# Perceiver layer on one core: half of the causal masks by ScalarE and GpSimd, one division for two quads, weights in halves, projections in four column groups

## The chip, the core and the metric

The kernel runs on one core of a Trainium2 chip. A core has five engines with a queue each: PE (TensorE, matmuls, and PEld for its weight loads), DVE (VectorE), ACT (ScalarE), POOL (GpSimd) and SP (SyncE, which issues most DMAs here). Each works through its own queue in order and waits on semaphores for the others. Matmul results land in PSUM[...]; what GpSimd works on here lies in SBUF. The metric is the device time of one execution in microseconds, as the median of several runs.

## The reference

x is 4 batches of 256 tokens with 256 features; the context is 4 x 4096 x 256. Everything is fp32. Three residual blocks follow each other:

```python
x = x + xattn(layernorm(x), ctx, ctx, ...)          # 16 heads of 16, 4096 keys, softmax
x = x + attn(layernorm(x), ...)                     # causal linear attention
x = x + ffn(layernorm(x), w_gate, w_up, w_down)     # silu(gate) * up, int32 weights / 127
```

The second block maps normalised queries and keys through 64 exponential features per head, and sums causally:

```python
kv_cur = jnp.cumsum(kv_prod, axis=2) + kv_state[:, :, None]
k_cur = jnp.cumsum(k_ch, axis=2) + k_state[:, :, None]
ctx = jnp.einsum('bhtf,bhtfd->bhtd', q_ch, kv_cur)
den = jnp.maximum(jnp.einsum('bhtf,bhtf->bht', q_ch, k_cur), 1e-06)
out_ch = ctx / den[..., None]
```

The kernel computes it as masked attention: for each head the scores of features against features, keys down and queries across, are set to zero where the key comes later, and then multiplied with the values and a column of ones, which gives the denominator.

## The kernel before, in words

**Cross-attention** (`cross_attention`, from L569) takes most of the time. Work is cut into units of one batch and one *quad* (four heads), 16 units of 16 steps each. A step works on 256 keys: matmuls for the maxima of a later unit (pm, L708, reduced by DVE at L715), the shifted scores (pt, L745), the exponentials on ACT (L750), and the product with the values (pav, L765), which DVE adds up at L775. In between, half of a key or value item is projected from the context (pk L642, pv L672). Each of these halves is written as matmuls of 32 output columns, four side by side: `pk[32 * j : 32 * j + 32, :]`. The trace shows such a matmul as two records of form 128*32, a full one as two of form 128*128, and one with 32 contraction rows as 32*128.

At the end of a unit, `finish` divides by the sums (`normalise`, L785), sends the rows through eight small DMAs on SP into another layout (xo<-on, L806), turns them (`turn`, px L815) and, for every second unit, projects them (`project`, py L823) and adds to the residual xr (L826).

**The causal part's beginning** is laid into the last steps of that loop (`start_causal`, L285): for batches 0 to 2, layernorm, transposition (tr L202), queries and keys (pqk L211, with the squares sq on GpSimd, L217), values (pv L229), normalisation of queries and keys (`qk_normed` L253, with `inverse_root`, L120, a chain of small DVE instructions), and the first features. Each of these calls uses two or four full 128-column matmuls.

**The causal part** (from L513) is an order written out by hand. It has 16 quads (`attend(n)`, n = 4 * batch + quad). Step n of the last loop queues, on all engines: `values` of quad n-1 (po L430, copied to avT by ACT, L435), `scores` of quad n (four heads, two at a time, pa L411 and L416, each masked by DVE: at = pa * mask, L421), `divide` of quad n-1 (two transpositions of avT into pt_o, L442, then den, reciprocal and product on DVE, L444 to L446), in steps 0, 2, 4, 8 and 10 `features` of two later quads (pf L275, clipped by DVE at L281, exponential by ACT at L282, a factor by GpSimd at L283), and then the step's entries in `fills`. These hold the conversion of the three int32 weights on ACT (`weight`, L394: steps 1, 2 and 3; each starts the load of the next on SP), the last unit's `turn15` and `project15` (steps 2 and 3), layernorm, queries, keys and values of batch 3 (norm3 in step 3, qk3 in 4 and 5, v3 in 5), and the output projection and feed-forward of each batch (tr_o L460, py L466, tr_z L483, pg and pu L492, pd L504) from step 4 on.

All PSUM tiles come from one pool of eight banks in turn (`bank`, L179), so a tile waits until the tile eight places earlier has been read.

```python
normalise()
weight_load(0)
fills[1] += [lambda: weight(0)]
fills[2] += [turn15, lambda: weight(1)]
fills[3] += [project15, norm3, lambda: weight(2)]
early = {0: 6, 2: 8, 4: 10, 8: 12, 10: 14}
```

## Time and profile before

| | |
|---|---|
| median of 3 runs | 1228.5 us (1228.21 to 1228.61) |
| profiled execution | 1229.02 us, its span 1227.3 us |
| PE / PEld busy | 1193.0 us (97%) / 807.0 us (66%) |
| DVE / ACT / POOL busy | 927.9 us (76%) / 673.0 us (55%) / 60.2 us (5%) |
| at<-pa,mask on DVE (L421) | 64 times, 550 ns each |
| at the end of the loop: last pav | 1065.9 to 1069.2 us |
| last instruction on DVE (o<-pd,xr) | 1224.1 us |

The span runs from the first to the last instruction of the profiled execution; the time of an execution includes what lies around it. An engine's busy time says nothing by itself of what a change is worth: the *chain* follows the work that ended last back to what released it, and shows which engine's time was the program's time at each place. Rows by stretch ("from:to length, PE busy (x instructions) ... PEclk, DMA share, GB/s") show where PE, which bounds the whole, has gaps. In a row of the timeline, the first number is the start, the second the duration, "x4" the number of instructions merged, and brackets hold the idle time before and what ended it.

### The profile page before, as it was taken

How to read it: one execution, taken by the hardware profiler on the slowest of the kernel's cores; microseconds unless marked ns; L12 is line 12 of the kernel's file. 1: busy time of each engine (PE TensorE's matmuls, PEld its weight loads, DVE VectorE, ACT ScalarE, POOL GpSimd, SP SyncE). 2: the span in 40 equal slices, each digit the busy share in tenths (PEclk: the TensorE clock that was granted, in tenths of full speed). 3: DMA queues.
4: the chain of work that ended last, by engine and by line, in shares of the span. 5: the costliest groups of instructions: out<-in, count | busy, mean ns of one | idle time of the engine just before them, and what ended most of it. 6: DMA issues, size and time to landing. Idle time of an engine off the chain costs nothing.

```text
span 1227.3 us, 42096 instructions
## 1 busy us (share of the span) xinstructions
PE 1193.0 (97%) x17712; PEld 807.0 (66%) x17712; DVE 927.9 (76%) x1823; ACT 673.0 (55%) x1394; POOL 60.2 (5%) x115
## 2 busy tenths in 40 slices
PE   7999999999999999999999999999999999959998
PEld 3566667666766676667666776677667755536777
DVE  6887777777777777777777777777788877577763
ACT  3456665566666655666656556655566546641311
POOL 4010000000000000000000000000001012120100
PEclk9999999999999999999999999999999999999999
DMA  6452331233123322332233213322232000020000
GB/s 208 135 192 67 101 114 56 80 105 106 64 79 89 116 71 63 103 119 72 60 102 106 86 58 91 103 90 73 86 105 91 5 1 4 2 80 1 10 9 18
DMA packets 57756, 95.78 MB, mean 78 GB/s; under 512 B 29024, under 2 KB 31712, under 8 KB 57568
## 3 DMA queue, kind: packets, MB, share of 16 engines
q1 hardware_dynamic: 56640, 92.44, 24.3%
q8 instruction: 140, 2.29, 0.8%
q10 hardware_dynamic: 416, 0.66, 0.2%
q14 instruction: 48, 0.39, 0.1%
q0 software_dynamic: 512, 0.00, 0.0%
HBM read 74.17 MB, written 1.05 MB: 61 GB/s over the span
## 4 chain that ended last, share of the span: by engine, by line
PE 92%; DVE 4%; ACT 1%; DMA 1%; issue 1%; SPq 0%; POOL 0%; DVEq 0%; ACTq 0%
PE pt L745 22%; PE pm L708 18%; PE pav L765 18%; PE pk L642 11%; PE pv L672 10%; PE pd L504 2%; PE pg L492 1%; PE pu L492 1%; PE pq L848 1%; PE pqk L211 1%; PE po L430 1%; PE pa L411 1%; PE py L823 1%; PE py L466 1%; DVE mx L715 1%; PE pf L275 1%
## 5 line engine op out<-in xcount | busy, mean ns | idle before, releaser
L715 DVE TENSOR_REDUCE mx<-pm 128x1 f32<-128x512 f32 x1024 | 635.6, 684 | 145.4 <-PE pm L708 145.3
L750 ACT ACTIVATE e<-pt 128x512 f32<-128x512 f32 x1024 | 529.2, 602 | 384.2 <-PE pm L708 359.6
L745 PE MATMUL pt<-qa,kt 32*128 32x256 f32 x4096 | 500.2, 388 | 1.3 <-DVE av L775 0.7
L708 PE MATMUL pm<-kt,qT 32*128 32x512 f32 x2048 | 494.6, 616 | 0.0
L745 PEld LDWEIGHTS pt<-qa,kt 32*128 32x128 f32 x4096 | 317.0, 184 | 117.2 <-ACT v L679 43.2
L765 PE MATMUL pav<-e,v 128*32 128x256 f32 x4096 | 269.8, 380 | 0.0
L708 PEld LDWEIGHTS pm<-kt,qT 32*128 32x128 f32 x2048 | 172.2, 184 | 15.5 <-issue 3.7
L765 PEld LDWEIGHTS pav<-e,v 128*32 128x32 f32 x4096 | 128.7, 110 | 73.9 <-ACT e L750 4.7
L775 DVE TENSOR_TENSOR av<-pav,av 128x256 f32<-128x256 f32 x240 | 101.7, 424 | 65.7 <-PE pav L765 65.4
L672 PE MATMUL pv<-wv_sb,ctx 128*32 128x128 f32 x4096 | 137.5, 276 | 0.0
L642 PE MATMUL pk<-ctx,wk_sb 128*32 128x256 f32 x2048 | 136.7, 388 | 0.0
L672 PEld LDWEIGHTS pv<-wv_sb,ctx 128*32 128x32 f32 x4096 | 104.2, 109 | 43.5 <-DVE mx L715 42.7
L642 PEld LDWEIGHTS pk<-ctx,wk_sb 128*32 128x32 f32 x2048 | 54.8, 110 | 67.1 <-DVE mx L715 39.0
L650 ACT ACTIVATE ku<-pk,bk_sb 128x256 f32<-128x256 f32 x128 | 63.2, 495 | 11.2 <-PE pk L642 9.9
L679 ACT COPY v<-pv 128x256 f32<-128x256 f32 x128 | 51.4, 402 | 9.9 <-PE pv L672 9.9
L802 POOL TENSOR_TENSOR on<-on,bv_sb 128x64 f32<-128x64 f32 x32 | 9.2, 308 | 820.5 <-DVE on L797 820.5
L421 DVE TENSOR_TENSOR at<-pa,mask 128x384 f32<-128x384 f32 x64 | 31.2, 550 | 7.0 <-PE pa L416 7.0
L282 ACT ACTIVATE kt<-kt,shift 128x512 f32<-128x512 f32 x32 | 22.4, 725 | 22.0 <-DVE kt L281 22.0
L281 DVE TENSOR_SCALAR kt<-pf,low,top 128x512 f32<-128x512 f32 x32 | 23.7, 803 | 3.9 <-PE pf L275 3.9
L492 PE MATMUL pg<-zT,wg 128*128 128x256 f32 x96 | 23.0, 382 | 0.7 <-ACT zT L484 0.7
L496 ACT ACTIVATE th<-pg 128x512 f32<-128x512 f32 x12 | 7.1, 594 | 29.8 <-PE pg L492 29.8
L492 PE MATMUL pu<-zT,wu 128*128 128x256 f32 x96 | 22.7, 379 | 0.0
(126 smaller groups left out, 565.6 us busy)
## 6 DMA issues: line engine op xcount, KB each, us to landing
ctx<-in_ctxT_dram SPq DMA_DIRECT2D x128, 512.0 KB
kt<-ku SPq DMA_DIRECT2D x508, 32.0 KB
xo<-on SPq DMA_DIRECT2D x128, 8.0 KB
xr<-in_x_dram SPq DMA_DIRECT2D x4, 256.0 KB
out_dram<-o SPq DMA_DIRECT2D x8, 128.0 KB
wqkv_sb<-in_wqkv_dram SPq DMA_DIRECT2D x1, 768.0 KB
w_i<-in_w_gate_dram SPq DMA_DIRECT2D x1, 768.0 KB
w_i<-in_w_up_dram SPq DMA_DIRECT2D x1, 768.0 KB
```

Source lines behind the costliest of these rows:

```text
L421: nc.vector.tensor_tensor(at, pa, mask, ALU.mult)
L492: nc.tensor.matmul(ps[:, i, :], lhsT=w[:, k, ns], rhs=zT[:, k, :], start=k == 0, stop=k == KC - 1)
L642: nc.tensor.matmul(pk[32 * j : 32 * j + 32, :], lhsT=wk_sb[:, k, m * P + 32 * j : m * P + 32 * j + 32], rhs=x[:, k, cs], start=k == 0, sto ...
L650: nc.scalar.activation(ku[:, cs], made.pop(), AF.Identity, bias=bk_sb[:, m : m + 1])
L672: nc.tensor.matmul(pv[32 * j : 32 * j + 32, i, :], lhsT=x[:, k, t0 + 32 * j : t0 + 32 * j + 32], rhs=wv_sb[:, k, m * P : (m + 1) * P], sta ...
L679: nc.scalar.copy(to.rearrange("p t (h d) -> p t h d", d=HD + 1)[:, :, :, :HD], made.pop().rearrange("p t (h d) -> p t h d", d=HD),)
L708: nc.tensor.matmul(pm, lhsT=qT[rows, q, t0 : t0 + P], rhs=kt[rows, c * CH : (c + 1) * CH], start=True, stop=True,)
L715: nc.vector.tensor_reduce(mx[:, i, j, c : c + 1], pm, AX.X, ALU.max)
L745: nc.tensor.matmul(pt[:, i, :], lhsT=kt[rows, ks], rhs=qa[rows, :], start=True, stop=True)
L750: nc.scalar.activation(e, pt, AF.Exp, scale=0.25)
L765: nc.tensor.matmul(pav[32 * h : 32 * h + 32, :], lhsT=v[:, t % KT, c0 : c0 + 32], rhs=es[n, h][:, i, :], start=i == 0, stop=i == 1,)
L775: nc.vector.tensor_tensor(avs[u], pav, avs[u], ALU.add)
```

## The change

Four things are changed.

1. A helper `product4` issues one product as four matmuls of 32 output columns each. pk and pv of the loop, which already did this, call it; new is that pqk (L211), pv of the causal part (L229) and py of the cross-attention (L823) do too.
2. Each int32 weight is loaded and converted in two halves, through a tile with two buffers. Two loads are queued after `normalise()`; the six conversions stand in steps 1 to 6, and each queues the load two places further on.
3. `divide` runs in every second step, for two quads: four transpositions into one bank, one den, reciprocal and product with twice the elements. avT gets three buffers.
4. Of the four scores of a quad, the first two are copied from PSUM by ACT, and GpSimd sets the two triangles of the copy to zero (`affine_select` over the blocks 0 and 2); the other two are multiplied by the mask on DVE as before.

The instructions of the other parts, and their order, stay as they are.

```diff
+    def product4(out, lhsT, rhs, **flags):
+
+        for j in range(4):
+            js = slice(32 * j, 32 * j + 32)
+            nc.tensor.matmul(out[js], lhsT=lhsT[:, js], rhs=rhs, **flags)
...
-                nc.tensor.matmul(
-                    ps, lhsT=zT[:, k, i * P : (i + 1) * P], rhs=rest[3][:, k, : 2 * D],
+                product4(
+                    ps, zT[:, k, i * P : (i + 1) * P], rest[3][:, k, : 2 * D],
                     start=k == 0, stop=k == KC - 1,
                 )
...
-                    nc.tensor.matmul(
-                        ps[:, i, :], lhsT=zT[:, k, i * P : (i + 1) * P], rhs=rest[3][:, k, 2 * D :],
+                    product4(
+                        ps[:, i, :], zT[:, k, i * P : (i + 1) * P], rest[3][:, k, 2 * D :],
                         start=k == 0, stop=k == KC - 1,
                     )
...
+    def weight_load(n):
+        i, half = divmod(n, 2)
+        w = ws[i].shape[1] // 2
+        src = (w_gate, w_up, w_down)[i][:, half * w : half * w + w, :]
+        coming[n] = work.tile([P, w, ws[i].shape[2]], I32, tag="w_i", name="w_i")
+        nc.sync.dma_start(out=coming[n], in_=src)
+
+    def weight(n):
...
+        nc.scalar.activation(
+            ws[i][:, half * w : half * w + w, :], coming.pop(n), AF.Copy, scale=(1.0, 0.5, 1.0)[i] / 127.0
+        )
+        if n + 2 < 6:
+            weight_load(n + 2)
...
                 for pa in pas:
                     at = work.tile([P, 3, P], F32, tag="at", name="at", bufs=8)
-                    nc.vector.tensor_tensor(at, pa, mask, ALU.mult)
+                    if part == 0:
+                        nc.scalar.copy(at, pa)
+                        nc.gpsimd.affine_select(
+                            out=at[:, 0:3:2, :], in_=at[:, 0:3:2, :], compare_op=ALU.is_ge, fill=0.0, base=0,
+                            pattern=[[0, 2], [1, P]], channel_multiplier=-1,
+                        )
+                    else:
+                        nc.vector.tensor_tensor(at, pa, mask, ALU.mult)
                     ats.append(at)
...
         def divide():
...
+            pt = bank([P, 2, 8, 32], "pt_o")
+            for m, oT in enumerate(got):
+                for i in range(2):
+                    nc.tensor.transpose(
+                        pt[:, i, 4 * m : 4 * m + 4].rearrange("p j r -> p (j r)"), oT[:, i * P : (i + 1) * P], ident
+                    )
+            got.clear()
+            den = work.tile([P, 2, 8], F32, tag="den", name="den")
             nc.vector.tensor_scalar(den, pt[:, :, :, HD], 1e-6, None, ALU.max)
             nc.vector.reciprocal(den, den)
...
-        weight_load(0)
+        for n in range(2):
+            weight_load(n)
...
+        for n in range(6):
+            fills[n + 1] += [lambda n=n: weight(n)]
+        fills[2] += [turn15]
+        fills[3] += [project15, norm3]
...
-            if n > 0:
+            if n > 0 and n % 2 == 0:
                 steps[n - 1][2]()
...
-                    nc.tensor.matmul(
-                        py, lhsT=oT[:, k, :], rhs=rest[1][:, k, :], start=k == 0, stop=k == KC - 1
-                    )
+                    product4(py, oT[:, k, :], rest[1][:, k, :], start=k == 0, stop=k == KC - 1)
```

More of the change, by code (lines that the diff above doesn't have):

```diff
@@ L363, in perceiver_layer @@
     finish = cross_attention(
-        tc, xr, load_x, load_rest, ctxT, wq_sb, bq_sb, wkP, bk_sb, wvP, eps, ident, layernorm, transposed,
+        tc, xr, load_x, load_rest, ctxT, wq_sb, bq_sb, wkP, bk_sb, wvP, eps, ident, layernorm, transposed, product4,
         qT, kts, lnp, bank, rest, start_causal)
@@ L386, in perceiver_layer @@
     ]
-    coming = []
-    def weight_load(i):
-        src = (w_gate, w_up, w_down)[i]
-        coming.append(load(src, list(ws[i].shape), "w_i", mybir.dt.int32, nc.sync, late))
-    def weight(i):
-        nc.scalar.activation(ws[i], coming[i], AF.Copy, scale=(1.0, 0.5, 1.0)[i] / 127.0)
-        if i + 1 < len(ws):
-            weight_load(i + 1)
+    coming = {}
+    def weight_load(n):
[5 more added lines that the diff above has]
+    def weight(n):
+        i, half = divmod(n, 2)
+        w = ws[i].shape[1] // 2
+        nc.scalar.activation(
[3 more added lines that the diff above has]
+            weight_load(n + 2)
+    got = []
     def attend(n):
         b, q = divmod(n, NQ)
-        ats, got = [], []
+        ats = []
         def scores():
@@ L433, in values @@
                     )
-            oT = work.tile([P, T], F32, tag="avT", name="avT")
+            oT = work.tile([P, T], F32, tag="avT", name="avT", bufs=3)
             nc.scalar.copy(oT, po)
@@ L438, in divide @@
         def divide():
-            oT = got.pop()
-            pt = bank([P, 2, 4, 32], "pt_o")
-            for i in range(2):
-                nc.tensor.transpose(pt[:, i].rearrange("p j r -> p (j r)"), oT[:, i * P : (i + 1) * P], ident)
-            den = work.tile([P, 2, 4], F32, tag="den", name="den")
+            pt = bank([P, 2, 8, 32], "pt_o")
[6 more added lines that the diff above has]
+            den = work.tile([P, 2, 8], F32, tag="den", name="den")
             nc.vector.tensor_scalar(den, pt[:, :, :, HD], 1e-6, None, ALU.max)
@@ L446, in divide @@
             nc.vector.tensor_tensor(
-                att[:, 2 * b : 2 * b + 2, 64 * q : 64 * q + 64].rearrange("p t (j d) -> p t j d", d=HD),
-                pt[:, :, :, :HD], den.unsqueeze(3).to_broadcast([P, 2, 4, HD]), ALU.mult,
+                att[:, 2 * b : 2 * b + 2, 64 * q - 64 : 64 * q + 64].rearrange("p t (j d) -> p t j d", d=HD),
+                pt[:, :, :, :HD], den.unsqueeze(3).to_broadcast([P, 2, 8, HD]), ALU.mult,
             )
@@ L519, in perceiver_layer @@
         norm3, turn3, qk3, sq3, v3, _ = causal_in(3)
-        fills[1] += [lambda: weight(0)]
-        fills[2] += [turn15, lambda: weight(1)]
-        fills[3] += [project15, norm3, lambda: weight(2)]
+        for n in range(6):
+            fills[n + 1] += [lambda n=n: weight(n)]
+        fills[2] += [turn15]
+        fills[3] += [project15, norm3]
         fills[4] += [turn3, lambda: qk3(0)]
@@ L569, in cross_attention @@
 def cross_attention(tc, xr, load_x, load_rest, ctxT, wq_sb, bq_sb, wkP, bk_sb, wvP, eps,
-                    ident, layernorm, transposed, qT, kts, lnp, bank, rest, start_causal):
+                    ident, layernorm, transposed, product4, qT, kts, lnp, bank, rest, start_causal):
     nc = tc.nc
@@ L640, in half @@
                 for k in range(KC):
-                    for j in range(4):
-                        nc.tensor.matmul(
-                            pk[32 * j : 32 * j + 32, :],
-                            lhsT=wk_sb[:, k, m * P + 32 * j : m * P + 32 * j + 32], rhs=x[:, k, cs],
-                            start=k == 0, stop=k == KC - 1,
-                        )
+                    product4(
+                        pk, wk_sb[:, k, m * P : (m + 1) * P], x[:, k, cs], start=k == 0, stop=k == KC - 1
+                    )
             def out(part):
@@ L670, in half @@
                     for k in range(KC):
-                        for j in range(4):
-                            nc.tensor.matmul(
-                                pv[32 * j : 32 * j + 32, i, :], lhsT=x[:, k, t0 + 32 * j : t0 + 32 * j + 32],
-                                rhs=wv_sb[:, k, m * P : (m + 1) * P], start=k == 0, stop=k == KC - 1,
-                            )
+                        product4(
+                            pv[:, i, :], x[:, k, t0 : t0 + P], wv_sb[:, k, m * P : (m + 1) * P],
+                            start=k == 0, stop=k == KC - 1,
+                        )
             def out(part):
@@ L822, in project @@
                 for k in range(KC):
-                    nc.tensor.matmul(
-                        py, lhsT=oT[:, k, :], rhs=rest[1][:, k, :], start=k == 0, stop=k == KC - 1
-                    )
+                    product4(py, oT[:, k, :], rest[1][:, k, :], start=k == 0, stop=k == KC - 1)
                 nc.vector.tensor_tensor(xr[:, t, :], py, xr[:, t, :], ALU.add)
```

## The prediction

> **What bounds the kernel now.** I read the page first (its slices, its chain), then busy time by stretches, then the chain and the engines' own timelines between 960 and 1228 us. The page's chain is 92% PE, and up to slice 35 PE is busy nine tenths or more: in the cross-attention loop, time is PE time, and only PE work taken out there counts. The end is different:

> ```profile
> core 0: us, PE busy (x) PEld busy (x) DVE busy (x) ACT busy (x) POOL busy (x), PEclk, DMA share, GB/s
> 130.00:900.00 770.00, 769.26 (x12659) 520.94 (x12652) 591.14 (x1054) 469.09 (x986) 7.45 (x26) 1.00 0.29 88
> ...
> 1080.00:1100.00 20.00, 11.78 (x118) 7.73 (x114) 14.13 (x44) 8.00 (x10) 3.42 (x6) 0.91 0.29 100
> 1100.00:1120.00 20.00, 15.96 (x106) 10.42 (x104) 14.04 (x40) 4.86 (x9) 3.99 (x6) 0.91 0.00 1
> 1120.00:1140.00 20.00, 19.37 (x143) 14.63 (x141) 18.04 (x47) 4.65 (x8) 1.41 (x3) 1.00 0.00 1
> ```

> From 1080 to 1120 PE idles 12.3 of 40 us and its clock is 0.91. Steps 0 to 7 of the causal part lie in 1070 to 1132; after that PE is full again (19.1 to 19.8 of 20 until 1200). The chain there, in order of time, says who holds PE up:

> ```profile
> 1077.67 4.33 DMA w_i<-in_w_gate_dram
> 1082.03 1.48 ACT wg L394
> 1083.51 0.27 ACT avT L435
> 1083.82 0.69 PE pt_o L442 x2
> 1084.51 2.06 PE pf L275 x16
> ...
> 1090.24 1.47 ACT wu L394
> 1091.70 0.27 ACT avT L435
> 1092.02 0.44 PE pt_o L442 x2
> 1092.45 0.88 PE py L823 x4
> ...
> 1098.01 1.86 DVE at L421 x4
> ...
> 1100.50 2.88 DVE kt L281 x4
> 1103.38 0.61 DVE zT L203
> 1104.03 3.68 PE pqk L211 x4
> ```

> A weight conversion on ScalarE waits for its DMA, the small copy avT waits behind it, the transposition pt_o waits for avT, and everything behind pt_o on PE waits too. Then VectorE is the chain, up to pqk, and again up to 1123.8, where values (po) takes 2.23 us instead of 0.86 because the masks come late. Two operations are also slow by themselves: pf 2.06 (1.07 at 1134.82) and pqk 3.68 (1.91 to 1.98 for the same two matmuls earlier). By stretches the granted clock is 0.50 from 1084 to 1086 and 0.53 from 1104 to 1106: 2.8 us lost, after PE pauses of 3.59 and 3.79 us.

> **Part 1, projections in column groups.** The same shape stands in the trace as pk and pav:

> ```profile
> 237.13 1.00 PE pk L642 x16
> 238.13 0.86 PE pav L765 x16
> 239.00 1.06 PE py L823 x4
> ```

> pk and pav are 8 calls of 32 columns each (two records a call), py two calls of 128; all stream the same number of columns. pav directly after pk costs 0.86; after a 32-row operation or a full 128-column one (at 985.82, 990.66, 996.59) it costs 1.00. The switch of form costs, not the number of calls. So py goes from 1.06 to 0.86 behind pav: 7 times 0.20 in the loop. pqk (1.91 to 1.98) plus pav (1.00) becomes 1.00 + 0.86 + 0.86 = 2.72: 6 times 0.23. L229's pv (1.92) plus pav becomes the same 2.72: 3 times 0.20. Sum 3.4; one pqk (1018) lies where VectorE is the chain (1016 to 1028), so I take **3.0**. [...] The row decides: 8 calls take 1.00, two take 1.06. Ends: 0 and 3.4.

> **Part 2, weights in halves.** SP still issues eight xo transfers first (until 1077.67), so the load starts no earlier. The whole load is seen after 4.36 us. By stretches of one us it moved at 276 and 406 GB/s from 1078.7 to 1080.7, so 393 KB are in at about 1080.0, and with the tail of 0.45 between the last bytes and ScalarE's start, the half is there at about 1080.5; the conversion halves to 0.74. avT of quad 1 then ends 1.5 + 0.7 = 2.2 us earlier. Ends: 0.7 (only the conversion) and 2.9. The other five halves have a whole step each for landing; the two buffers make SP wait, with nothing but later halves queued behind it until the first output.

> **Part 3, division for two quads.** Step 3 has no transposition any more. That was the wait of 2.57 us at 1092.02, for avT behind four exponentials and a whole conversion; py now waits only for the oT copy, behind VectorE's clips. The copy avT of quad 2 is needed a step later. Gain about 2.4 up to py. Transpositions stay 32 in number, 0.27 to 0.37 a pair; the form switch that is saved in even quads is paid by the next pg instead: nothing. VectorE saves 8 times den and reciprocal (0.16 + 0.20), off the chain except in steps 3 to 7.

> **Part 4, half of the masks.** VectorE loses 2 of 4 masks in each quad (pitch 0.465). ScalarE gains two copies 128x384 from PSUM: avT (128x256) takes 0.37, zT (128x512) 0.59, so 0.48 each. GpSimd gains two selects of 2x128. The nearest row is the mask's own making:

> ```profile
> 1069.77 0.54 POOL L375 TENSOR_SCALAR_AFFINE_SELECT mask<-mask 128x128 f32<-128x128 f32 x2
> ```

> 0.27 for 128 elements; for 256, between 0.4 (a fixed part as in L283, 0.48 for 256) and 0.54; I take 0.45. So these masks come about 0.9 us after the scores instead of 0.47, but a step is 6 us long, and values reads them a step later. What is queued behind the copies on ScalarE are avT, exponentials, conversions: 0.84 a step on an engine that is a quarter busy from 1100 on. In steps 1 and 3 the copies stand behind four exponentials (ended 1076.7 and 1090.3): po then waits about 3.1 and 2.0 us where it waited less, but that time was lost at pt_o in any case.
> Walking the engines' orders with these durations, VectorE's chain in step 4 is shorter by two masks less a longer division (0.7), form switches in step 5 give 0.2, and step 7's late masks vanish (0.63 wait + 1.4 stretch, 2.2 with their switch).

> **A price.** [...]

> ```profile
> 1020.92 2.13 DVE L253 TENSOR_TENSOR kt<-kt,nrm 128x512 f32<-128x512 f32 x2
> ...
> 1021.14 1.35 POOL L217 TENSOR_TENSOR sq<-kt 128x512 f32<-128x512 f32 x1 [10.05 <-DVE kt L215]
> ```

> against 1.28 and 1.04 apart. The selects of quad 3 fall into the root's small steps of norm3 (L131 to L133, two inputs), which are the chain: by the row 0.85[...]; I take **0.9** off. Ends 0 and 2. [...] The feed-forward's roots have some 3 us before their z is turned (tr_z stands behind 5.2 us of pd); the root of normed in step 5 has less, which is in the upper end.

> **Sum.** Up to py 2.2 + 2.4, less 0.1 for a changed wait: 4.5. Step 4: 0.7. Step 5: 0.2. Step 7: 2.2. That is 7.6. Less 0.9. Loop 3.0. The half clock cost 2.8; the pause before pqk stays about 3.7 us by the same walk, the first falls into pieces of 3.1 and 0.8; I count one short relapse of 1.0, so 1.8 won. Total 7.6 - 0.9 + 3.0 + 1.8 = **11.5 us**. The profiled execution took 1229.0 (span 1227.3), so 1217.5; the median of the runs is 0.5 lower: **1217.0**.

> **Rivals.**
> *The clock and the handover eat the middle.* Both pauses still bring the half clock (-1.8)[...]: 8.6 won, 1219.9. For it: the pause before pqk hardly shrinks. Against: shorter stalls of 2.57 and 2.06 left the clock at 1.00.
> *Column groups give nothing*[...], or the loop hides them: 8.5 won, 1220.0. For it: the loop's VectorE is busy three quarters. Against: the 0.14 between the two costs of pav.
> *GpSimd decides; slower.* All 32 masks pass it, in one strict order with 20 multiplications by fac, each 0.48, that the scores need. If a select of this two-block pattern costs 2 us instead of 0.45, two selects and the features fill the 6 us step and everything from step 2 on follows GpSimd: the walk's 7.6 is gone at 2.0 us, and with the loop's 3.0 the tie with before lies at 2.2; at 2.5 the end comes 8 us later than now in the causal part, 1228.5 + 8 - 3 = 1233.5. For it: spans on POOL are rough, and no row has this shape. Against: five times the nearest row.
> *The change doesn't do what it says*: the masks are needed so late that only PE counts, and weights land as late as before: about 1225.

> **Chances.** Forecast 0.64, clock and handover 0.13, no column gain 0.11, little of it 0.05, GpSimd 0.05, no change 0.02. Everything won (3.4 + 7.7 + 2.8) gives 1214.6; loop 1.0, middle 5.6, no clock gives 1222. Range 1214 to 1222. A difference under 0.2% (2.5 us) can't be told from none; faster 0.92, same 0.03, slower 0.05.

> **What will show it.** pav after pqk at 0.86 and py at 0.86; ScalarE's first conversion starting near 1080.5 less the loop's gain; no pt_o in odd steps and py about 5 us nearer to the loop's end; po of step 7 without a stretch; selects of about 0.45; clock 1.00 in the middle. Wrong would be: selects over 1 us, po waiting for GpSimd after step 8, or a loop that ends no earlier.

## The result, and the profile after

The changed kernel takes **1217.6 us** (median of 4 runs, 1216.87 to 1217.84) against 1228.55 for the kernel before on the same chip (4 runs, 1228.21 to 1228.62). The ratio is 0.991 with a 95% interval of 0.9893 to 0.9927: 11.0 us less, where 11.5 were forecast. The profiled execution took 1217.58 us with a span of 1215.9, 11.4 shorter than the span before.

The stretches of the causal part, in the same columns as before:

```profile
1080.00:1100.00 20.00, 13.87 (x132) 7.78 (x131) 14.33 (x38) 10.87 (x19) 7.87 (x15) 0.91 0.23 68
1100.00:1120.00 20.00, 19.95 (x194) 14.39 (x193) 17.84 (x54) 6.97 (x14) 3.39 (x7) 1.00 0.01 2
1120.00:1140.00 20.00, 19.44 (x160) 15.13 (x158) 13.60 (x37) 6.92 (x14) 3.48 (x8) 1.00 0.02 7
```

PE idles 6.2 us between 1080 and 1120, half of the 12.3 before (6.5, if the stretches are laid 2.8 us earlier, as the loop now ends), and of the two stretches with a clock of 0.91 one is left. GpSimd's busy time (the fifth pair) has more than doubled in the first row, from 3.42 to 7.87, without becoming full. The chain of waits over the same steps, shortened to the lines that answer to those of before:

```profile
1073.93 3.15 DMA w_i<-in_w_gate_dram
...
1077.85 0.36 ACT avT L458
...
1078.26 0.44 PE pt_o L465 x2
1078.69 1.11 PE pf L281 x16
...
1083.14 1.11 PE py L159 x16
...
1090.85 2.88 DVE kt L287 x4
1093.72 0.61 DVE zT L209
...
1094.38 3.46 PE pqk L159 x16
```

pt_o of quad 1 starts at 1078.26 instead of 1083.82, pf is back from 2.06 to 1.11, and py starts at 1083.14 instead of 1092.45 with no transposition just ahead of it. But pqk, two stages later, still takes 3.46, and VectorE is still the chain ahead of it. The timeline gives the same place from the side of the waits and of the new operations. First two rows of the kernel before, then the changed one:

```profile
1104.03 3.68 PE L211 MATMUL pqk<-wqkv_sb,zT 128*128 128x512 f32 x4 [3.79 <-DVE zT L203]
...
1123.78 2.23 PE L430 MATMUL po<-at,va 128*32 128x256 f32 x16 [0.63 <-DVE at L421]
```

```profile
1068.87 0.78 POOL L439 TENSOR_SCALAR_AFFINE_SELECT at<-at 128x256 f32<-128x256 f32 x2
...
1074.88 1.23 PE L453 MATMUL po<-at,va 128*32 128x256 f32 x16 [2.44 <-POOL at L439]
...
1077.10 0.84 ACT L405 ACTIVATE wg<-w_i 128x768 f32<-128x768 int32 x1 [2.36 <-DMA w_i<-in_w_gate_dram]
...
1085.42 1.23 PE L453 MATMUL po<-at,va 128*32 128x256 f32 x16 [1.21 <-POOL at L439]
...
1094.38 3.46 PE L159 MATMUL pqk<-wqkv_sb,zT 128*32 128x512 f32 x16 [3.97 <-DVE zT L209]
...
1113.40 1.00 PE L453 MATMUL po<-at,va 128*32 128x256 f32 x16
```

A select takes 0.39 us (two in 0.78). po waits for GpSimd twice, for 2.44 and 1.21 us, and no longer waits in step 7, where it took 2.23 after a wait of 0.63 and now takes 1.00. The pause before pqk is 3.97 us, no shorter than before (3.79).

Where the 11.4 us of span went is found by laying both executions side by side at five events:

| stretch | before | after | won | forecast |
|---|---|---|---|---|
| start to the end of the last pav (loop) | 1069.21 | 1066.43 | 2.8 | 3.0 |
| to the start of py | 23.24 | 16.71 | 6.5 | 4.5, and 1.0 of the clock (pf) |
| py to the start of pqk (step 4) | 11.58 | 11.24 | 0.3 | 0.7 - 0.9 = -0.2 |
| pqk itself | 3.68 | 3.46 | 0.2 | 0.8 of the clock |
| end of pqk to the end | 119.59 | 118.06 | 1.5 | 0.2 (step 5) + 2.2 (step 7) = 2.4 |

The last column shares out the prediction's terms; of its clock term of 1.8, pf's return from 2.06 to 1.1 is put where pf stands. Two rows hold some chance. The end of the loop differs by up to 0.9 us between executions with the same loop (1070.08 in e2_halves below, 1069.21 here). And in the profiled execution of the kernel before, SP was held up longer ahead of the first weight than in any other; the timeline has the eight xo transfers of the kernel before, of the changed one, and of e3_divide below, which still loads whole weights:

```profile
1071.32 6.25 SPq L806 DMA_DIRECT2D xo<-on  x8
```

```profile
1068.54 5.28 SPq L830 DMA_DIRECT2D xo<-on  x8
```

```profile
1072.15 5.28 SPq L811 DMA_DIRECT2D xo<-on  x8
```

In all thirteen other profiles they take 5.28 us. So about 1.0 of the 6.5 us belongs to this one execution before and not to the change, and 5.6 is left for the 5.5 that were forecast. The medians give 11.0 for the whole.

### The profile page after: what moved, and what is told of

Same layout as the page of the kernel before. It is cut to its first block, busy times and chain, and to the rows that moved or that the text cites. A ratio compares the mean times of both kernels' runs of the same rounds, so it can differ in the third digit from the quotient of the medians.

```text
span 1215.9 us, 42635 instructions
## 1 busy us (share of the span) xinstructions
PE 1187.2 (98%) x18000; PEld 801.0 (66%) x18000; DVE 911.6 (75%) x1767; ACT 686.8 (56%) x1429; POOL 72.7 (6%) x147
## 4 chain that ended last, share of the span: by engine, by line
PE 93%; DVE 5%; ACT 1%; DMA 1%; issue 0%; DVEq 0%; ACTq 0%
PE pt L769 22%; PE pm L732 18%; PE pav L789 18%; PE pv L159 11%; PE pk L159 11%; PE pd L530 2%; PE pg L518 2%; PE pu L518 1%; PE pq L870 1%; PE pqk L159 1%; PE pa L427 1%; PE py L492 1%; DVE kt L287 1%; DVE mx L739 1%; PE py L159 1%; PE po L453 1%
## 5 line engine op out<-in xcount | busy, mean ns | idle before, releaser
L444 DVE TENSOR_TENSOR at<-pa,mask 128x384 f32<-128x384 f32 x32 | 16.3, 551 | 14.2 <-PE pa L432 14.1
L530 PE MATMUL pd<-wd,hT 128*128 128x256 f32 x96 | 21.6, 381 | 0.0
```

What stands on the lines that cost most here:

```text
L530: nc.tensor.matmul(pd, lhsT=hT[:, n, i * P : (i + 1) * P], rhs=wd[:, n, :], start=n == 0, stop=n == NH - 1)
```

## The experiments

Every kernel computes the same outputs. In the tables, "before" is measured in the same session as the kernel beside it.

### One part at a time

Four kernels are the one before with a single part of the change: the three calls of `product4`; the weights in halves; the common division; the copies and selects for two of four masks.

```diff
 e1_projections (three such places)
-                nc.tensor.matmul(
-                    ps, lhsT=zT[:, k, i * P : (i + 1) * P], rhs=rest[3][:, k, : 2 * D],
+                product4(
+                    ps, zT[:, k, i * P : (i + 1) * P], rest[3][:, k, : 2 * D],
 e2_halves
-        weight_load(0)
+        for n in range(2):
+            weight_load(n)
...
+        for n in range(6):
+            fills[n + 1] += [lambda n=n: weight(n)]
 e3_divide
-            if n > 0:
+            if n > 0 and n % 2 == 0:
 e4_masks
-                    nc.vector.tensor_tensor(at, pa, mask, ALU.mult)
+                    if part == 0:
+                        nc.scalar.copy(at, pa)
+                        nc.gpsimd.affine_select(
...
+                    else:
+                        nc.vector.tensor_tensor(at, pa, mask, ALU.mult)
```

> The kernel before with only the projections in four column groups (pqk, L229's pv and py). Theory: what costs is the switch of form, so the loop ends 2.8 us earlier, as its last pav did in the changed kernel, the causal part stays as it was (both lapses of the clock included), and the median falls from 1228.5 to about 1225.7. Rival (four times the calls cost what the saved switches give): 1227.5 or more.

> The kernel before with only the weights loaded and converted in halves. Theory: avT of quad 1 comes 2.5 us earlier, and avT of quad 2 has half a conversion less ahead of it (0.7); the first pause of PE falls under 1.5 us, so the first lapse of the clock goes too (1.0): 3.8 us in all, about 1224.7. Rival (the wait only moves to the next transposition, which stands behind four exponentials anyway): 1 us or less, 1227.5.

> The kernel before with only the division for two quads. Theory: PE's wait of 2.57 us for avT of quad 2 goes, but the whole conversion still holds avT of quad 1, and VectorE's chain takes part of it back: 1.7 us, the first lapse of the clock may stay: about 1226.8. Rival (every transposition left out is a stall left out): 3 us or more, 1225.5.

> The kernel before with only half of the masks by ScalarE and GpSimd. Theory: nothing until step 3, where ScalarE and not VectorE is late; 0.9 us in step 4 and 2 us in step 7: 2.9 us, about 1225.6, with both lapses of the clock still there. Rival[...]: 1 us or less, 1227.5.

| | median (runs) | before | ratio, 95% | won alone |
|---|---|---|---|---|
| e1_projections | 1225.09 (10) | 1227.92 | 0.9976, 0.9966 to 0.9985 | 2.8 |
| e2_halves | 1225.91 (9) | 1227.92 | 0.9981, 0.997 to 0.9991 | 2.0 |
| e3_divide | 1228.80 (12) | 1227.92 | 1.000, 0.9991 to 1.0008 | -0.9, not told from 0 |
| e4_masks | 1226.72 (20) | 1227.92 | 0.9989, 0.9982 to 0.9996 | 1.2 |

The projections bring alone what the loop won in the changed kernel. The others fall short of what was expected of them, and the sum of the four is 5.1 us, not 11. The chain of e3_divide shows how a part that removes a wait of 2.57 us can bring so little:

```profile
1090.94 5.58 DMA w_i<-in_w_down_dram
...
1097.93 0.36 ACT avT L437
...
1098.34 0.69 PE pt_o L444 x2
1099.03 2.06 PE pf L275 x16
```

Step 3 has no transposition and PE runs on; but the next one, of step 4, needs the avT of the quad just behind it, and this copy stands on ScalarE behind the conversion of the third weight, which waits for its load. PE then idles 4.66 us ahead of pt_o instead of 2.57 and 2.06 in two places, and the clock falls, to 0.53 between 1098 and 1100: pf takes 2.06 again, as it did at 1084.51 in the kernel before. In this execution it stays at one half for 10.24 us from 1098.12, and it was at one half for 3.41 us in the loop too, from 1029.85. Its granted clock is 0.993, against 0.997 in the profiled execution before; but over all runs the means are 0.994 and 0.995, so the clock can explain only a part. With the weights in halves that load has landed by then. In the same way e4_masks keeps its three waits for avT (3.02, 1.97 and 2.04 us) and e2_halves, which cuts the first from 3.59 to 0.77, keeps a wait of 2.18 for the next and one of 3.79 ahead of pqk. Each of them frees PE up to the next wait.

### One part left out

If waits stand behind each other, a part must be worth more as the last one added than as the first. Two kernels are the changed one without the masks' move, and without the common division.

```diff
 e10_no_masks
-                    if part == 0:
-                        nc.scalar.copy(at, pa)
-                        nc.gpsimd.affine_select(
...
-                    else:
-                        nc.vector.tensor_tensor(at, pa, mask, ALU.mult)
+                    nc.vector.tensor_tensor(at, pa, mask, ALU.mult)
 e11_no_common_division
-            if n > 0 and n % 2 == 0:
+            if n > 0:
```

> The changed kernel with all masks on VectorE again. Theory (each part is worth more where the others have removed the other waits): 3.4 us slower, 1221.0, from step 4 (one us) and step 7 (two). Rival (what the part gave alone, 1.2, is what it gives): 1218.8.

> The changed kernel with one division a quad again. Theory (py and the chain of norm3 wait for avT of quad 2 again): 2.2 us slower, 1219.8. Rival (alone the part gave nothing, so it gives nothing here): 1217.6.

| | median (4 runs each) | before | ratio, 95% | last part is worth | alone |
|---|---|---|---|---|---|
| e10_no_masks | 1221.13 | 1228.56 | 0.9941, 0.9926 to 0.9956 | 3.5 | 1.2 |
| e11_no_common_division | 1220.81 | 1228.56 | 0.9936, 0.9922 to 0.9951 | 3.2 | -0.9 |

By the medians both are worth more at the end than alone. Their values (median less 1217.59) come from runs of different sessions, in which the kernel before differed by 0.01 us. In e11 PE waits 2.12 us for avT and 4.59 ahead of pqk; in e10 1.44 for a mask ahead of pf and 3.53 ahead of pqk, and the half clock lasts 6.83 and 10.24 us, against 3.41 in the changed kernel. So part of these values is clock. An estimate from these traces: PE is busy for 3.14 us of the half-clock stretch in the changed kernel, for 4.56 in e11 and for 6.67 in e10; if half of that is lost, 0.7 of the 3.2 and 1.8 of the 3.5 are clock. What is left for the division, 2.5, is clearly more than its -0.9 alone; for the masks, 1.7 against 1.2, it is too near to tell.

### The price of the selects

```diff
 e5_selects_twice
                             pattern=[[0, 2], [1, P]], channel_multiplier=-1,
                         )
+                        nc.gpsimd.affine_select(
+                            out=at[:, 0:3:2, :], in_=at[:, 0:3:2, :], compare_op=ALU.is_ge, fill=0.0, base=0,
+                            pattern=[[0, 2], [1, P]], channel_multiplier=-1,
+                        )
```

> The changed kernel with every select on GpSimd done twice over, with the same output. Theory (GpSimd has room, values come a step later): steps 2 and 4, where po waits for the select, lose up to 0.8 us each, and since other waits stand there too, about 1 us in all: 1218.6. Rival (GpSimd is about to decide): 0.8 us more in most of the 16 steps, 1224 or more.

It took 1219.95 us (4 runs, 1219.56 to 1220.61; before 1228.33; ratio 0.9929, 0.9914 to 0.9943): 2.4 above the changed kernel. So neither the selects nor the time that they cost VectorE (below) are free, but they are far from deciding the time. po's two waits went from 2.44 and 1.21 to 2.37 and 1.68, with a second one of 0.21 and 0.23 inside each. What was not expected is a second half-clock stretch of 3.41 us from 1076.55, all of it under a busy PE, where half the clock loses 1.7 us; the other now starts at 1097.03. Taking these 1.7 off would leave 0.7, near the 1 us expected. But the one of its runs with a granted clock of 0.999, like most of the changed kernel's, still took 1219.56, so how much of the 2.4 is clock stays open.

What selects cost VectorE can be read in the changed kernel itself, where a pair of selects runs beside the root of a layer norm (timeline, both engines):

```profile
1102.94 0.78 POOL L439 TENSOR_SCALAR_AFFINE_SELECT at<-at 128x256 f32<-128x256 f32 x2 [3.21 <-ACT at L438]
...
1103.04 0.31 DVE L132 SCALAR_TENSOR_TENSOR ir_t<-ir_t,ln_v 128x2 f32<-128x2 f32 x1
1103.39 0.34 DVE L133 SCALAR_TENSOR_TENSOR ir_y<-ir_t,ir_y 128x2 f32<-128x2 f32 x1
```

Elsewhere these two take 0.16 to 0.17, so two selects cost this engine 0.33 us together, less than one select lasts. On the root of the queries' and keys' norms, at 1109.55, it is 0.25 (0.32 and 0.38 in the chain, 0.21 and 0.24 in the kernel before). The masks show no such cost: two on VectorE take 1.01 at 1089.01 in the changed kernel, where GpSimd works on xr from 1088.92 to 1090.37, and 1.01 at 1105.60, where it is idle.

### The half clock ahead of pqk

pqk takes 3.46 us after a pause of 3.97. Two ways to cover the pause were tried, and one to shorten it. e6_pe_kept_busy repeats the four transpositions of z of that batch to 20, e9_transposes_in_pause to 28; e8_matmuls_in_pause adds 12 matmuls by the identity, with the same result in the same bank. e7_features_later moves `features(10)` and with it VectorE's four clips of kt from step 4 to step 7, behind the copy zT that pqk waits for.

```diff
 e6_pe_kept_busy (e9: 7 in place of 5)
-            for i in range(2):
+            for i in list(range(2)) * (5 if b == 3 else 1):
 e8_matmuls_in_pause
+            for i in list(range(2)) * (3 if b == 3 else 0):
+                for k in range(KC):
+                    nc.tensor.matmul(
+                        ps[:, k, i, :], lhsT=z[:, i, k * P : (k + 1) * P], rhs=ident, start=True, stop=True
+                    )
 e7_features_later
-        early = {0: 6, 2: 8, 4: 10, 8: 12, 10: 14}
+        early = {0: 6, 2: 8, 7: 10, 8: 12, 10: 14}
```

> The changed kernel with the four transpositions of z of batch 3 done five times over into the same place, 1.7 us more work for PE in its pause ahead of pqk, with the same output. Theory (the half clock of pqk comes from the pause): pqk takes 1.75 instead of 3.46, the clock stays 1.00, 1.7 us faster: about 1215.9. Rival (the slow pqk is something else, or the added work delays zT): 1217.6 or slower.

> The changed kernel with the features of quads 10 and 11 in step 7 instead of step 4, so that VectorE's four clips (2.9 us) no longer stand ahead of the copy zT for which PE pauses. Theory: the pause ahead of pqk falls from 4 to under 2 us, 1.2 us are kept after step 7 takes the clips, and the half clock of pqk goes (1.7): 2.9 us, about 1214.7. Rival (step 7 has no room on VectorE either, its masks and qT come late again): 1217 or slower.

> The changed kernel, where after the four transpositions of z of batch 3 the same result is written three times more by 12 full matmuls with the identity: some 2.6 us more of matmuls in PE's pause ahead of pqk, with the same output. Theory[...]: no half clock at pqk, 1.75 us for it instead of 3.46, about 1215.9. Rival (a clock that follows the total of PE's work in the part, or pqk slow by itself): pqk as before, 1217.6.

> The same pause filled for as long (2.6 us) by 24 more transpositions instead of matmuls, with the same output. Theory[...]: the half clock stays, pqk 3.46, about 1217.6. Rival (any work of PE keeps the clock; the earlier run with 16 more simply covered too little of the pause): pqk 1.75, about 1215.9.

| | median (4 runs each) | before | ratio, 95% | pause | pqk |
|---|---|---|---|---|---|
| after | 1217.59 | 1228.55 | 0.991, 0.9893 to 0.9927 | 3.97 | 3.46 |
| e6_pe_kept_busy | 1217.93 | 1228.33 | 0.9908, 0.9894 to 0.9923 | 2.22 | 3.50 |
| e8_matmuls_in_pause | 1216.53 | 1228.56 | 0.9904, 0.9888 to 0.9921 | 1.29 | 1.92 |
| e9_transposes_in_pause | 1216.55 | 1228.56 | 0.9902, 0.9887 to 0.9917 | 1.35 | 1.93 |
| e7_features_later | 1214.89 | 1228.33 | 0.9892, 0.9876 to 0.9909 | 1.92 | 1.92 |

Pause and pqk are those of the profiled execution. e6 missed: the clock fell all the same, in three of its four runs (1217.75 to 1218.27); the fourth kept a clock of 1.00 and took 1215.94, as expected. Two readings of it stood: that its transpositions, whatever their number, left the clock to fall, or that 16 of them covered too little (the pause was still 2.22 us). e8 and e9 fill the pause for equally long, 2.6 us by estimate, one with matmuls, one with transpositions. e9, whose timeline follows, decided for the second. A row by stretch stands below it:

```profile
1090.89 3.27 PE L208 MATMUL tr<-ident,z 128*128 128x128 f32 x28
...
1095.51 1.93 PE L159 MATMUL pqk<-wqkv_sb,zT 128*32 128x512 f32 x16 [1.35 <-DVE zT L209]
```

```profile
1092.24:1095.66 3.42, 2.07 (x22) 1.83 (x24) 3.22 (x5) 2.92 (x5) 1.43 (x3) 1.00 0.00 0
```

Twenty-eight fp32 transpositions keep pqk at 1.93 as well as matmuls do. Of PE's 2.07 us in that stretch 1.92 are transpositions, and the clock stayed at 1.00 behind it. (This execution has a half-clock stretch elsewhere, in the loop from 1027.39, and at 1217.16 it is one of the two slower runs of e9; those at a clock of 1.00 took 1215.61 and 1215.93.) Both fillers take time of their own (zT has to wait for the last of them), and their medians lie only 1.0 us under the changed kernel's, within overlapping intervals; what is shown is the duration of pqk.

e7 takes the cause away rather than covering it. In its chain zT comes directly behind the division, without the clips between:

```profile
1089.70 0.42 DVE att L472
1090.13 0.61 DVE zT L209
...
1090.78 1.92 PE pqk L159 x16
```

The pause is 1.92, the clock stays at 1.00 through the causal part, and the median is 2.7 under the changed kernel's (its runs go from 1214.33 to 1216.92, the intervals overlap). Its span is 3.3 us shorter, of which 0.7 lies in the loop, which is the same in both.

### A faster version

e12_two_orders adds to e7 that `features(12)` and `features(14)` come a step later, and the six conversions too.

```diff
-            fills[n + 1] += [lambda n=n: weight(n)]
+            fills[n + 2] += [lambda n=n: weight(n)]
...
-        early = {0: 6, 2: 8, 4: 10, 8: 12, 10: 14}
+        early = {0: 6, 2: 8, 7: 10, 9: 12, 11: 14}
```

> The changed kernel with another order: features of quads 10, 12 and 14 in steps 7, 9 and 11 (instead of 4, 8 and 10), and each conversion of half a weight one step later, so that none stands ahead of avT of quad 1. Theory: as with the features later (1214.9), less 0.5 at the first transposition and 0.5 in step 8, where ScalarE's exponentials no longer stand ahead of the copies oT: about 1213.8. Rival (only the pause ahead of pqk mattered): 1214.9.

1215.14 us (4 runs, 1213.53 to 1215.89; before 1228.73; ratio 0.989, 0.9874 to 0.9907). The profiled span is 0.8 us shorter than e7's, but the median is not lower, and the 1213.8 expected was missed. Whether the second order helps stays open; either of the two is the fastest version run, about 1215 us.

## Why the prediction held

**Projections, 3.0: right, 2.8.** The forecast rested on two durations of pav, 0.86 and 1.00. In the chain of the loop before, and then of the changed one:

```profile
983.83 1.98 PE pqk L211 x4
985.82 1.00 PE pav L765 x16
...
991.67 1.06 PE py L823 x4
```

```profile
982.82 1.93 PE pqk L159 x16
984.75 0.86 PE pav L789 x16
...
990.26 0.86 PE py L159 x16
```

pqk in 8 calls takes no longer than in two (1.85 to 1.93 on the chain, before 1.91 to 1.98; the forecast had 1.00 + 0.86), pav behind it 0.86 instead of 1.00, and py behind pav 0.86 instead of 1.06. e1 gives 2.8 on its own.

**Weights in halves, 2.2: right in mechanism, somewhat too large.** pt_o of quad 1 came 2.8 nearer to the loop's end (11.83 us behind it instead of 14.61). But 1.0 of that is the slow xo transfers in the profiled execution before: its load was issued 8.46 us after the loop's end, that of the changed kernel 7.50, and so were the whole loads of e1, e3 and e4. "The load starts no earlier" was right. From its issue, the half was seen after 3.17 us instead of 4.36, a gain of 1.2 where 1.5 were reckoned; the conversion takes 0.84, not 0.74, and avT behind it 0.36 instead of 0.27. From issue to pt_o that makes 1.8 (6.15 before, 4.33 after).

**Common division, 2.4 up to py: right in the sum, wrong as a price of its own.** Step 3 has no pt_o. Of the 6.5 us that py comes nearer, 2.8 lie ahead of pt_o and 1.2 are the clock in pt_o and pf; 2.5 are left for the division, about as forecast. But this gain exists only beside the other parts: alone the division gave -0.9, as the last one 3.2. The prediction walked all parts at once, and that is why its sum held; its terms are not prices of the parts.

**Masks: right in mechanism.** Selects of 0.39 for an estimated 0.45, ScalarE's copies of 0.43 for 0.48; po waits of 2.44 and 1.21 for 3.1 and 2.0. Step 7 lost its 1.9 us of wait and stretch, but the end of pqk to the end won 1.5 where 2.4 were forecast; where the rest went was not followed.

**Selects beside VectorE's root, -0.9: mis-sized.** The prediction took 0.9 off, close to the 0.85 by which its row shows kt lengthened beside sq; its rival with the clock added 1.1, up to the upper end of 2.0. In norm3 the selects fell on the pair of z, which takes 0.90 instead of the 0.73 of the kernel before: 0.17. Where they fall on the root (1103) it is 0.33.

**The clock, +1.8: mis-sized.** One relapse, as forecast, but it costs 1.5 (pqk 3.46 against 1.93 in e9), not 1.0. Before, pf lost 1.0, pt_o 0.25 and pqk 1.7; so some 1.4 was won. The pause ahead of pqk, forecast at 3.7, is 3.97. The prediction judged the clock by the length of a pause alone. But a pause of 2.57 us left it at 1.00 in the kernel before (at 1092.02), and one of 2.22 did not in e6: by my reading, where a pause falls among the stretches of the last section counts too.

**The total, 11.5: in part luck.** The two mis-sized terms nearly cancel: 0.7 too much off for the selects beside VectorE, 0.4 too much on for the clock. And in the rows of the table behind py, 2.1 were won (0.3, 0.2 and 1.5) where 3.0 were forecast (-0.2, 0.8 and 2.4), which the slow xo transfers of the one execution before made good; by the medians the forecast is 0.5 too high.

GpSimd did not decide, as forecast from a row with half of the pattern; e5, with two selects for each, still lies 8 us under the kernel before.

## What to carry over

Price an edit by what waits directly behind the stall that it removes: of four parts that bring 11 us together, three brought between -0.9 and 2.0 alone, and their chains show PE running on to the next wait. Look at which work of VectorE stands in front of the one copy that TensorE waits for, and move that before you fill the gap: the median of the reordering in e7 lies 2.7 us under the changed kernel's, those of the two fillers that kept the clock 1.0. Count changes of tile form in a stream of matmuls, not only the calls: behind pqk in column groups pav took 0.86 us, behind the full pqk 1.00.

## What the hardware showed beyond that

```profile
1090.69:1094.11 3.42, 0.00 (x0) 0.00 (x0) 3.42 (x6) 2.51 (x4) 1.21 (x3) 1.00 0.00 0
1094.11:1097.52 3.41, 3.14 (x16) 0.59 (x16) 0.21 (x1) 1.10 (x2) 0.70 (x2) 0.50 0.35 100
```

```profile
1090.90:1094.31 3.41, 1.39 (x13) 1.15 (x11) 3.41 (x6) 2.58 (x4) 1.28 (x3) 1.00 0.00 0
1094.31:1097.73 3.42, 3.22 (x16) 0.60 (x16) 0.14 (x1) 1.04 (x2) 0.63 (x2) 0.50 0.38 105
```

e6's transpositions made PE 41% busy in the stretch ahead (1.39 of 3.41), and half clock followed all the same. It followed behind 0.00 and 0.11 us of PE in the kernel before, 0.00 in the changed one, 1.00 in e1, 1.24 and 0.75 in e5; behind the 2.07 us of e9's row above it did not. I cut the kernel before and the changed one into such stretches, from 130 us on. Of 631 at full clock, three were followed by half clock (those with 0.00, 0.11 and 0.00 us of PE); in the other 628 PE was busy for 1.71 us or more, and full clock followed. The half-clock stretches of these two kernels, with PE busy for 3.25, 3.41 and 3.14 us, end after one length; that of e11 lasts two, with PE busy for 4.56 of 6.83 us, that of e10 three, with 6.67 of 10.24. The two stretches in the loop, in e3 (from 1029.85) and e9 (from 1027.39), are not explained. PE's busy time in a trace is partly modelled, so these figures are rough, and no run was made to find where between 1.39 and 1.71 us the change lies.

**The relapse doesn't start at the same place in every execution.** From the loop's end it starts after 27.68 us in the changed kernel and 27.84 in e6; in e10 after 24.74, and one length later is 28.15 there, 0.5 us later than in the changed kernel. An estimate from these figures: a pause between 2.0 us (3.41 less e6's 1.39) and 3.4 costs 1.5 us in some executions and none in others. The clocks of single runs bear this out in part: e6 took 1215.94 us at a clock of 1.00 and 1217.75 to 1218.27 at 0.997 to 0.999; e9 1215.61 and 1215.93 at 1.00, 1217.16 and 1217.70 at 0.998; e7 1214.33 to 1215.13 at 1.00, 1216.92 at 0.998; e3 1225.65 and 1225.66 at 0.996, 1226.69 to 1229.54 at 0.992 to 0.994. In e1 (1224.12 to 1226.05 at 0.997) and e8 (1215.77 to 1217.46 at 1.00) the clock doesn't order the runs, so it isn't the whole of the spread.
